# Layer 1's values by way of DRAM: tokens on partitions, and v's bias folded into the output's bias

## The chip, the cores and the metric

The kernel runs on one core of one Trainium2 chip. The metric is the device time of one execution in microseconds (us), as the median of several runs. The core's engines are TensorE (PE), VectorE (DVE), ScalarE (ACT), GpSimd (POOL) and SyncE (SP); in this kernel SP issues every DMA.

## What is computed

Thirty-two batches of 128 rows by 1024 columns pass through two layers, each an attention-like step and a low-rank expert step, each added to the running `x`:

```python
x = x + _L0_xattn_ref(_layernorm(x), ctx, ctx)       # autocorrelation along the 128 rows
x = x + _L0_ffn_ref(_layernorm(x), ...)              # dense 1024x1024 + 8 experts of rank 16, top 2
x = x + _L1_xattn_ref(_layernorm(x), ctx, ...)       # windowed attention along the 1024 columns
x = x + _L1_ffn_ref(_layernorm(x), ...)              # 4 experts of rank 16, top 2
```

The change lies in the third line. There the 128 rows are channels (8 heads of 16) and the 1024 columns are tokens. Queries come from `x`, keys and values from the context of the batch:

```python
q = Wq @ x + bq ;  k = Wk @ ctx + bk ;  v = Wv @ ctx + bv
k, v = zero padding of 8 tokens before, 7 after
for each head, token t: attn = softmax(q[t] . k[t-8 .. t+7] / 4); out[t] = sum attn * v[t-8 .. t+7]
return Wo @ out + bo
```

The padding is of zeros after the bias, so a padded token has the value 0 and not bv.

## The kernel before

**A planner sets the order.** `mk_kernel` doesn't issue instructions directly. Calls on V, A, G, PE and SP (DVE, ACT, POOL, PE, SP) are recorded as operations with a cost, the tiles they use and the earlier operations they depend on (`Planner._record`, `_touch`, `_cost`). `Planner.plan` then simulates the five engines and at each step gives a free engine its ready operation of the best priority: the batch number times a period, less the operation's remaining path, less a bias of its stage. The biases, the number of batches that may be open at a time (`win`), margins and a second set for the last part of the run stand in `CFG["plan"]`. Each engine gets its instructions in the order found; on the chip it runs them in that order, and each waits for what it needs. `emit` (line 363) issues them all, so every instruction has line 363 in the profile, and tiles tell them apart.

**Buffers.** Work tiles come from classes of fixed slots: `u` (128 x 512 f32, 43 of them), `p` (the 8 PSUM banks), `d` (128 x 1024 f32, 2), and small ones (`m`, `s`, `t`, `r`). A batch's inputs take six `u`: two halves each of `x`, of the context, and of the context split into two f16 parts. Constants and `k16`, `vpad`, `qbd` and `vbd` are there once and shared by all batches.

**A batch** passes the stages load, spec, corr, top, wt, inv (layer 0's autocorrelation, twice, for each half of the columns), ffn0 with gate and base, then kv, q, S, PV, wo (layer 1's attention) and ffn1. Several batches are open at once. The first operations of the run prepare the weights (stages setup and ws): the dense weights are loaded, their maxima found, and they are scaled and split into `wsp`.

**Products in three parts.** Most products are in f16 with each operand as a high and a low part; `three` adds high x high, high x low and low x high in one PSUM bank.

**Values before.** In `attention`, for each half of 512 tokens, `three(p, wv16, c16[g])` gives the values with channels on partitions and tokens along the row. ACT scales them and adds the bias into a `u`; ACT copies the high part into `vpad`, POOL subtracts to get the low part (`split`). `vpad` (128 x 1040 x 2 f16) holds high and low part side by side, with padding that stays zero. The product P x V needs tokens on partitions, in overlapping blocks of 32 tokens for every 16 queries. Four DVE transposes of 32 x 32 squares of 32-bit words (each word a high and a low part) per batch write them into `d` tiles. Eight DMAs copy from there into `vbd`, four for each half, one for each group of 32 channels; `vbd` is block diagonal by heads and is the stationary operand of the matmuls of stage PV. `qbd` is filled by eight DMAs for each half in the same manner from the queries, and is the stationary operand of stage S. `vbd` and `qbd` hold one half at a time.

**After PV** `eh` scales the result (each channel has its own scale for its values), `woT` multiplies it, and one DVE instruction adds `bo` and the running x (stage wo).

Of the kernel before, what the change touches and what calls it, by code (L numbers as in the profile page):

```python
# [14 lines left out]
F16 = mybir.dt.float16  # L15
# [7 lines left out]
S = 128  # L23
# [2 lines left out]
EPS = 1e-5  # L26
NEG = -3.0e38
TINY = 1e-30
CFG = {'nu': 43, 'nd': 2, 'en': 'G', 'cl': 'G', 'xl': 'G', 'sm': 'V', 'sw': 'A', 'wg': 'VG', 'q0': 'G', 'ns': 28, 'nt': 48, 'plan': {'phases': [{'at': 0.0, 'T': 19.88, 'margin': 178, 'win': 5, 'su': 60, 'sp': 3, 'ru': 1, 'rp': 0, 'bias': {'kv': -5.1, 'load': 10.0, 'S': -6.7, 'gate': 38.6, 'ffn1': 7.4, 'q': 0.4, 'top': 1.3, 'PV': -5.6, 'inv': 3.4, 'wt': 4.5, 'spec': 5.4, 'wo': 41.4, 'ws': -9.4, 'base': -1.7, 'ffn0': 90.1, 'corr': 5.4, 'setup': -12.6}}, {'at': 1459.1, 'T': 30.14, 'margin': 69, 'win': 6, 'su': 57, 'sp': 1, 'ru': 2, 'rp': 1, 'bias': {'kv': -32.9, 'load': -45.0, 'S': 18.4, 'gate': 125.0, 'ffn1': -67.8, 'q': 29.1, 'top': -23.6, 'PV': -37.2, 'inv': 57.1, 'wt': -20.7, 'spec': -56.0, 'wo': -29.3, 'ws': -71.2, 'base': -21.0, 'ffn0': 60.9, 'corr': -125.0, 'setup': 2.0}}], 'slack': [1.013, 0, 0]}}
NTOP = int(2 * math.log(S))  # L30
X_SC = 2.0 ** 10
W_SC = 2.0 ** 14
# [8 lines left out]
class _View:  # L41
# [24 lines left out]
    def broadcast_to(self, shape):  # L66
        return self._step("broadcast_to", shape)

    def windows(self, n, step, width):
        return self._step("__getitem__", (slice(None), slice(0, 1)))._wrap(n, step, width)  # L70

    def _wrap(self, n, step, width):
        f = lambda ap: bass.AP(ap.tensor, ap.offset, [list(ap.ap[0]), [step, n], [1, width]])
        return _View(self.tile, f(self.proto), self.path + ((f, None, None),))
# [7 lines left out]
    def region(self):  # L82

        ap = self.proto
        size = mybir.dt.size(ap.dtype)
        dims = [list(d) for d in ap.ap]
        row = dims[0][0]
        p0, f0 = divmod(ap.offset, row)
        last = f0 + sum(s * (n - 1) for s, n in dims[1:])
        return p0, p0 + dims[0][1], f0 * size, (last + 1) * size  # L90


class _Tile:
    def __init__(self, cls, slot=None, const=False):
        self.cls, self.slot, self.const = cls, slot, const
        self.log, self.users = [], {}


class _Op:
# [6 lines left out]
class Planner:  # L106
# [72 lines left out]
    def _cost(self, op, method, v, kw):  # L179
# [21 lines left out]
        if eng == "Activation":  # L201
            op.dur += (n + (61 if src.proto.space == PSUM else 112)) / 1.2 + 94 * (nsc + ("accum_out" in v))
            if src.region()[0] != out.region()[0]:
                op.dur += 127.0
            elif out.proto.ap[-1][0] > 1:
                op.dur += 0.2 * n
        elif eng == "DVE":
            n = max(n, size(src))
            two = method in ("tensor_copy", "tensor_scalar", "memset") and not psum and n > 64
            op.dur += 6 * n / 0.96 + 67 if method == "reciprocal" else (n * (0.5 if two else 1.0) + 64 + 59 * nsc) / 0.96  # L210
            op.dur += 70.0 * ("accum_out" in v) + {"match_replace": 67.0, "transpose": 25.0}.get(method, 0.0)
        elif eng == "Pool":
            small = mybir.dt.size(out.proto.dtype) == 2
            if method == "memset":
                op.dur += 40.0 + (0.85 if small else 0.2) * n
            else:
                rate = (2.8 if small else 1.2) if method == "tensor_scalar" else 1.88 if small else 2.1
                if any(x.proto.ap[-1][0] == 0 for x in v.values()) and n > 128:
                    rate = 1.67
                op.dur += 530.0 if kw.get("op") == ALU.pow else 150.0 + rate * n  # L220
        else:
            run = out.proto.ap[-1][1] * mybir.dt.size(out.proto.dtype)
            dram = any(x.tile is None for x in v.values())
            op.dur += (3200.0 if dram else 2900.0 if run > 128 else 3500.0) + out.shape[0] * n * mybir.dt.size(out.proto.dtype) / 360.0

            op.cold = 450.0 if dram else 720.0 if run > 128 else 840.0


    def _lat(self, a, b):
# [4 lines left out]
    def plan(self, phases, slack):  # L234
# [45 lines left out]
        while events:  # L280
            now = events[0][0]
            if phases and now >= phases[0][0]:
                period, window, margin, scarce, reserve, bias = phases.pop(0)[1]
                prio = lambda o: (period * max(o.batch, 0) - o.tail - bias.get(o.stage, 0.0), o.index)
                ready = {e: sorted((prio(o), o) for _, o in l) for e, l in ready.items()}
            while events and events[0][0] <= now:
                o = heappop(events)[2]
# [77 lines left out]

def plan_args(c):
    us = lambda v: v * 1e3
    scarce = lambda f: {"u": f["su"], "p": f["sp"], "d": 9, "m": 3, "r": 9, "s": 9, "t": 9}
# [6 lines left out]
def mk_kernel(ctx: ExitStack, tc: tile.TileContext, T: dict, out: bass.AP):  # L375
# [3 lines left out]

    cp = ctx.enter_context(tc.tile_pool(name="const", bufs=1))  # L380
    pp = ctx.enter_context(tc.tile_pool(name="psum", bufs=1, space=PSUM))

    def slot(name, shape, dt=F32):
# [98 lines left out]
    V.tensor_copy(bsum[:, 2:3], absb[:, 1:2])  # L482
    pb = B()
    PE.matmul(pb[:, 0:3], lhsT=blk1, rhs=bsum, start=True, stop=True)
    bqs, sq, bqsc, uq = (const(n, [128, 1]) for n in ("bqs", "sq", "bqsc", "uq"))
    V.tensor_scalar(bqs, pb[:, 0:1], TINY, 1.0 / W_SC, op0=ALU.add, op1=ALU.mult)
    V.reciprocal(sq, bqs)
# [4 lines left out]
    V.tensor_scalar(kvs[:, 1:2], rows[:, 2:3], C_SC / W_SC, None, op0=ALU.mult)  # L492
    V.tensor_scalar(kvb[:, 0:1], pb[:, 2:3], TINY, 1.0 / W_SC, op0=ALU.add, op1=ALU.mult)
    V.tensor_scalar(kvb[:, 1:2], absb[:, 2:3], TINY, 1.0 / W_SC, op0=ALU.add, op1=ALU.mult)
    V.tensor_scalar(rsx, rows[:, 1:3], 1.0 / W_SC, None, op0=ALU.mult)
    V.reciprocal(rsc, rsx)

    wqT = const("wqT", [128, 128])
# [321 lines left out]
    def attention(b, x, c16, m1, sums):  # L820
        P.stage = "kv"

        bd, skv, bsc, esc, usc, eh = s(2), s(2), s(2), s(2), s(1), s(2)
# [3 lines left out]
        G.tensor_tensor(bsc, bkv_raw, skv, op=ALU.mult)  # L827
# [39 lines left out]
        for g in range(2):  # L867
# [137 lines left out]
def _arrays(i):  # L1005
# [11 lines left out]
        "woT": a["L1_xattn_Wo"].T,  # L1017
# [22 lines left out]
```

## Time and profile before

| | |
|---|---|
| runs | 1600.08 us median (1599.47 to 1602.74, 3 runs) |
| the profiled execution | 1600.9 us, its span 1599.1 us |
| granted TensorE clock, mean | 0.974 |
| busy PE / DVE / ACT / POOL | 1520.9 / 1468.7 / 1417.8 / 1346.0 us |
| DMA engines, mean share | 48% (queue q1 47.8%), 142 MB in 854368 packets |
| matmuls | 19144 |

The span runs from the first to the last instruction. A busy share says how long an engine had an instruction in work, and nothing of whether another waited for it. For that there are the waits, by engine and by what ended them, and the chain of what ended last. By that chain PE holds 90% of the span, DVE 3%, ACT 2%, and the rest is in issue, DMA, POOL and SP's queue. In slices of 40 us, PE is at 9 tenths or more in all but the first two and the last two; DVE, ACT and POOL are at 8 or 9 tenths in nearly all between.

DMA pieces by size: 524288 of 32 bytes (into `qbd`), 262144 of 128 bytes (into `vbd`), 43712 of 2048 bytes (halves of 512 f32). Issuing one DMA holds SP for a median of 0.38 us (an input half) to 0.72 us (`qbd`).

### The profile page before, as it was taken

The numbers are of one execution on the slowest core, as the hardware profiler recorded it, in microseconds if no ns is written. First come the engines' busy times: TensorE is split into PE (matmuls) and PEld (weight loads), VectorE is DVE, ScalarE is ACT, GpSimd is POOL, SyncE is SP. The second block draws the span as 40 slices with busy tenths as digits, with TensorE's granted clock in tenths as the row PEclk, the third lists the DMA queues.
The fourth block names the chain that finished last, engine by engine and source line by source line (L and its number), as shares of the span: only waits on it lengthen the run. The fifth ranks groups of instructions, "written<-read, shape, count | busy, mean of one in ns | idle before, by whom it ended". The sixth has DMA issues, their size and how long they took to land.

```text
span 1599.1 us, 51794 instructions
## 1 busy us (share of the span) xinstructions
PE 1520.9 (95%) x19144; PEld 1001.9 (63%) x19144; DVE 1468.7 (92%) x5042; ACT 1417.8 (89%) x2833; POOL 1346.0 (84%) x1506
## 2 busy tenths in 40 slices
PE   2599999999999999999999999999999999999985
PEld 1256666666666666666666666666666666666654
DVE  6778999999999999999999999999999999999875
ACT  4998999999999999999999999999999999999753
POOL 5789878998888899888889988888998888899742
PEclk7789999999999999999999999999999999999996
DMA  8214544554454555445455544545455454554352
GB/s 267 81 56 57 98 63 91 102 105 91 91 91 70 94 102 106 91 91 92 69 96 101 105 91 92 93 68 96 100 105 92 90 95 68 95 100 78 41 70 58
DMA packets 854620, 145.72 MB, mean 91 GB/s; under 512 B 808224, under 2 KB 810528, under 8 KB 854368
## 3 DMA queue, kind: packets, MB, share of 16 engines
q1 hardware_dynamic: 854368, 142.41, 47.8%
q8 instruction: 152, 2.49, 0.7%
q14 instruction: 100, 0.82, 0.2%
HBM read 41.80 MB, written 16.78 MB: 37 GB/s over the span
## 4 chain that ended last, share of the span: by engine, by line
PE 90%; DVE 3%; ACT 2%; issue 1%; DMA 1%; POOL 1%; SPq 1%; POOLq 0%; DVEq 0%; ACTq 0%
PE p L363 90%; ACT u L363 2%; DVE u L363 1%; POOL u L363 1%; SPq L363 1%; DVE wsp L363 0%; DVE t L363 0%; DMA cf<-in_cf 0%; DVE s L363 0%; DMA u<-u 0%; DVE wmx L363 0%; DMA vbd<-d 0%; DVE mm L363 0%; DMA qbd<-u 0%; ACT k L363 0%
## 5 line engine op out<-in xcount | busy, mean ns | idle before, releaser
L363 POOL TENSOR_TENSOR u<-u,u 128x512 f32<-128x512 f32 (+1 forms) x640 | 774.9, 1233 | 94.4 <-ACT u L363 86.8
L363 PE MATMUL p<-wsp,u 128*128 128x512 f16 (+1 forms) x2304 | 409.9, 328 | 1.8 <-DVE r L363 0.9
L363 ACT ACTIVATE u<-p 64x512 f32<-64x512 f32 (+1 forms) x576 | 331.9, 591 | 52.0 <-PE p L363 43.7
L363 ACT ACTIVATE u<-u,t 128x512 f32<-128x512 f32 (+1 forms) x448 | 320.7, 723 | 62.3 <-DVE t L363 46.6
L363 DVE SCALAR_TENSOR_TENSOR u<-p,u 128x512 f32<-128x512 f32 (+1 forms) x448 | 289.2, 681 | 54.4 <-PE p L363 27.3
L363 PEld LDWEIGHTS <-u 128*128 128x128 f16 x3072 | 218.2, 98 | 167.0 <-issue 4.2
L363 ACT ACTIVATE u<-p,t 64x512 f32<-64x512 f32 (+3 forms) x448 | 265.7, 619 | 21.1 <-PE p L363 15.0
L363 PE MATMUL p<-u,ch 128*128 128x512 f16 x960 | 239.1, 385 | 1.9 <-DVE u L363 1.9
L363 PEld LDWEIGHTS <-qbd 128*128 128x128 f16 x6144 | 172.0, 96 | 27.1 <-issue 11.1
L363 PE MATMUL p<-k,qbd 128*128 128x32 f16 x6144 | 174.6, 176 | 1.6 <-issue 1.1
L363 PEld LDWEIGHTS <-ch 128*128 128x128 f16 x960 | 95.3, 102 | 120.7 <-issue 27.3
L363 PEld LDWEIGHTS <-vbd 128*128 128x128 f16 x6144 | 164.0, 97 | 8.5 <-issue 1.4
L363 PE MATMUL p<-u,vbd 128*128 128x32 f16 x6144 | 164.4, 176 | 0.7 <-POOL u L363 0.7
L363 ACT ACTIVATE u<-u,t,t 128x512 f32<-128x512 f32 x192 | 144.0, 820 | 5.2 <-POOL t L363 5.2
L363 POOL TENSOR_TENSOR t<-t,mhalf 128x1 f32<-128x1 f32 x128 | 71.5, 558 | 79.4 <-DVE t L363 79.0
L363 POOL TENSOR_TENSOR u<-u,s 128x512 f32<-128x512 f32 x128 | 134.2, 1050 | 0.7
L363 PE MATMUL p<-u,cf 128*128 128x512 f32 x256 | 125.2, 611 | 10.0 <-POOL u L363 10.0
L363 DVE SCALAR_TENSOR_TENSOR u<-p,t,u 128x512 f16<-128x512 f32 (+1 forms) x192 | 106.0, 567 | 16.9 <-ACT u L363 8.7
L363 ACT ACTIVATE u<-u 128x512 f16<-128x512 f32 x194 | 117.3, 623 | 3.4 <-DVE u L363 3.3
L363 PE MATMUL p<-ident,u 128*128 128x128 f32 x768 | 104.4, 279 | 10.6 <-ACT u L363 10.5
L363 PEld LDWEIGHTS p<-ident,u 128*128 128x128 f32 x768 | 90.8, 144 | 22.5 <-ACT u L363 13.4
L363 ACT ACTIVATE u<-p,t,t 128x512 f32<-128x512 f32 x128 | 94.0, 775 | 0.3 <-PE p L363 0.3
(155 smaller groups left out, 2863.8 us busy)
## 6 DMA issues: line engine op xcount, KB each, us to landing
vbd<-d SPq DMA_DIRECT2D x256, 128.0 KB
u<-u SPq DMA_DIRECT2D x192, 128.0 KB
u<-in_ctx SPq DMA_DIRECT2D x64, 256.0 KB
u<-in_x SPq DMA_DIRECT2D x64, 256.0 KB
qbd<-u SPq DMA_DIRECT2D x512, 32.0 KB
out<-u SPq DMA_DIRECT2D x64, 256.0 KB
u<-u SPq DMA_DIRECT2D x64, 126.0 KB
u<-in_wbT SPq DMA_DIRECT2D x16, 256.0 KB
```

The source lines that it names most:

```text
L363: fn(*[f(a) for a in args], **{k: f(a) for k, a in kw.items()})
```

## The change

Values are computed with tokens on partitions. The roles of the matmul's operands are exchanged: 128 tokens of the context are the stationary operand and `wv16` (128 x 128) the moving one, four blocks of tokens per half. ACT and DVE write the high and the low part, side by side, straight from PSUM into one `u`; SP stores it in a DRAM tile of 1040 rows (tokens) by 256 f16. The eight DMAs into `vbd` read their blocks from there. There are two such tiles, for even and odd batches.

Since channels now lie along the row, one scale for all channels takes the place of a scale for each: the set-up finds the largest row sum and the largest bias (`gm`). The bias bv isn't added to the values. The attention's weights add up to 1, so it is a constant, and `Wo bv + bo` is made once (`bo2`). A padded token must then hold −bv in place of 0: ACT and POOL make that row (`pads`) for each batch, and two DMAs store it ahead of the first and behind the last token.

`vpad`, the `d` tiles and the `windows` view go, and `u` has 49 slots in place of 43. The planner's cost of a DMA and its other rules are as before for all operations in this kernel; a DRAM tile counts as one region, so each store into it is planned behind the one before, and each load behind the last store. A bias may now be given for a stage on one engine too. The plan's numbers are others throughout (window 6 batches in place of 5 in the first part, the second part's set from 1484.0 us of planned time in place of 1459.1, all biases).

```diff
-CFG = {'nu': 43, 'nd': 2, ... 'plan': {'phases': [{'at': 0.0, 'T': 19.88, 'margin': 178, 'win': 5, 'su': 60, 'sp': 3, ...
+CFG = {'nu': 49, ... 'plan': {'phases': [{'at': 0.0, 'T': 20.72, 'margin': 430, 'win': 6, 'su': 101, 'sp': 99, ...
...
+    def grid(self, offset, dims):
+        f = lambda ap: bass.AP(ap.tensor, ap.offset + offset, [list(d) for d in dims])
+        return _View(self.tile, f(self.proto), self.path + ((f, None, None),))
...
-                prio = lambda o: (period * max(o.batch, 0) - o.tail - bias.get(o.stage, 0.0), o.index)
+                prio = lambda o: (period * max(o.batch, 0) - o.tail - bias.get(o.stage, 0.0) - bias.get(o.stage + "/" + o.eng, 0.0), o.index)
...
-        "d": [slot(f"d{i}", [128, D]) for i in range(CFG["nd"])],
...
+    vd = []
+    for i in range(2):
+        vd.append(P.fixed(dp.tile([D + 16, 256], F16, tag=f"vd{i}", name=f"vd{i}")))
+        vd[i].tile.whole = True
...
-    vpad = keep("vpad", [128, D + 16, 2], F16, 0.0)
...
+    bvr, nbv, bo2 = U(), const("nbv", [16, 128]), const("bo2", [128, 1])
+    SP.dma_start(out=bvr[0:16, 0:128], in_=T["bvr"].broadcast_to([16, 128]))
+    V.tensor_scalar(nbv, bvr[0:16, 0:128], -1.0, None, op0=ALU.mult)
+    PE.matmul(pb[:, 264:265], lhsT=woT, rhs=bkv_raw[:, 1:2], start=True, stop=True)
+    V.tensor_scalar(bo2, pb[:, 264:265], bo, None, op0=ALU.add)
...
-            for i, (w, hi, lo) in enumerate(((wk16, k16[:, 0, sl], k16[:, 1, sl]), (wv16, vpad[:, sl, 0], vpad[:, sl, 1]))):
-                t, p = U(), B()
-                three(p, w, c16[g])
-                A.activation(t, p, AF.Identity, bias=bsc[:, i : i + 1], scale=esc[:, i : i + 1])
-                split(hi, lo, t, G)
-
-        words = vpad.bitcast(U32).rearrange("p n i -> p (n i)")
-        v16 = []
-        for g in range(2):
-            t = P.tile("d")
-            tv = t.bitcast(U32).rearrange("p (b c) -> p b c", c=32)
-            for h in range(2):
-                V.transpose(tv[:, h * 16 : (h + 1) * 16], words[:, (2 * g + h) * 256 :].windows(16, 16, 32))
-            v16.append(h16(t).rearrange("p (b c i) -> p b c i", b=32, i=2))
+            t, p = U(), B()
+            three(p, wk16, c16[g])
+            A.activation(t, p, AF.Identity, bias=bsc, scale=esc[:, 0:1])
+            split(k16[:, 0, sl], k16[:, 1, sl], t, G)
+
+        vb = vd[b % 2]
+        t, u = M(), M()
+        pads = h16(u).rearrange("p (n r) -> p n r", r=2)
+        A.activation(t[0:16], nbv, AF.Copy, scale=skv[0:16, 1:2])
+        A.activation(pads[0:16, :, 0], nbv, AF.Copy, scale=skv[0:16, 1:2])
+        G.tensor_tensor(pads[0:16, :, 1], t[0:16], pads[0:16, :, 0], op=ALU.subtract)
+        for i in range(2):
+            SP.dma_start(out=vb[i * (D + 8) : i * (D + 8) + 8], in_=h16(u)[8 * i : 8 * i + 8])
+        for g in range(2):
+            t, p = h16(U()), B()
+            with P.group():
+                for n in range(4):
+                    for i, (m, r) in enumerate(THREE):
+                        PE.matmul(p[:, n * 128 : (n + 1) * 128], lhsT=c16[g][:, m, n * 128 : (n + 1) * 128],
+                                  rhs=wv16[:, r], start=i == 0, stop=i == 2)
+            v = t.rearrange("p (n r) -> p n r", r=2)
+            A.activation(v[:, :, 0], p, AF.Copy, scale=esc[:, 1:2])
+            V.scalar_tensor_tensor(v[:, :, 1], p, esc[:, 1:2], v[:, :, 0], op0=ALU.mult, op1=ALU.subtract)
+            SP.dma_start(out=vb[8 + g * HALF : 8 + (g + 1) * HALF].rearrange("(n p) e -> p n e", p=128),
+                         in_=t.rearrange("p (n e) -> p n e", n=4))
...
-                SP.dma_start(out=vbd[hs, :, hs], in_=v16[g][hs])
+                SP.dma_start(out=vbd[hs, :, hs].rearrange("p b n r -> p b (n r)"),
+                             in_=vb.grid(g * HALF * 256 + 64 * hp, ((256, 32), (16 * 256, 32), (1, 64))))
...
-            V.scalar_tensor_tensor(x[g], p, bo, x[g], op0=ALU.add, op1=ALU.add, accum_out=sums[:, g : g + 1])
+            V.scalar_tensor_tensor(x[g], p, bo2, x[g], op0=ALU.add, op1=ALU.add, accum_out=sums[:, g : g + 1])
```

More of the change, by code (lines that the diff above doesn't have):

```diff
@@ L28 @@
 TINY = 1e-30
-CFG = {'nu': 43, 'nd': 2, 'en': 'G', 'cl': 'G', 'xl': 'G', 'sm': 'V', 'sw': 'A', 'wg': 'VG', 'q0': 'G', 'ns': 28, 'nt': 48, 'plan': {'phases': [{'at': 0.0, 'T': 19.88, 'margin': 178, 'win': 5, 'su': 60, 'sp': 3, 'ru': 1, 'rp': 0, 'bias': {'kv': -5.1, 'load': 10.0, 'S': -6.7, 'gate': 38.6, 'ffn1': 7.4, 'q': 0.4, 'top': 1.3, 'PV': -5.6, 'inv': 3.4, 'wt': 4.5, 'spec': 5.4, 'wo': 41.4, 'ws': -9.4, 'base': -1.7, 'ffn0': 90.1, 'corr': 5.4, 'setup': -12.6}}, {'at': 1459.1, 'T': 30.14, 'margin': 69, 'win': 6, 'su': 57, 'sp': 1, 'ru': 2, 'rp': 1, 'bias': {'kv': -32.9, 'load': -45.0, 'S': 18.4, 'gate': 125.0, 'ffn1': -67.8, 'q': 29.1, 'top': -23.6, 'PV': -37.2, 'inv': 57.1, 'wt': -20.7, 'spec': -56.0, 'wo': -29.3, 'ws': -71.2, 'base': -21.0, 'ffn0': 60.9, 'corr': -125.0, 'setup': 2.0}}], 'slack': [1.013, 0, 0]}}
+CFG = {'nu': 49, 'en': 'G', 'cl': 'G', 'xl': 'G', 'sm': 'V', 'sw': 'A', 'wg': 'VG', 'q0': 'G', 'ns': 28, 'nt': 48, 'plan': {'phases': [{'at': 0.0, 'T': 20.72, 'margin': 430, 'win': 6, 'su': 101, 'sp': 99, 'ru': 1, 'rp': 0, 'bias': {'kv': -4.1, 'load': 10.2, 'S': -7.0, 'gate': 17.9, 'ffn1': 12.4, 'q': 11.5, 'top': 1.0, 'PV': -2.0, 'inv': 9.8, 'wt': 4.2, 'spec': 3.8, 'wo': 159.2, 'ws': 15.4, 'base': -0.4, 'ffn0': 56.4, 'corr': 5.2, 'setup': -7.3, 'q/SP': -14.9, 'setup/PE': 22.2, 'S/Activation': 1.9, 'load/DVE': 2.1, 'ffn1/PE': -11.8, 'corr/DVE': 13.7, 'q/Pool': 18.1, 'wt/DVE': 15.0, 'load/SP': 6.8, 'inv/Activation': 2.0, 'ffn1/DVE': 47.1, 'ffn0/Pool': -42.4, 'ffn1/Pool': 60.0, 'wo/DVE': 42.4, 'ws/SP': 21.8, 'gate/Activation': -17.3, 'load/Pool': -14.7, 'wo/PE': 3.6, 'ws/Pool': -14.6, 'wt/Activation': 6.4, 'ffn0/PE': 18.9, 'corr/PE': 3.1, 'setup/SP': 7.9, 'top/Activation': -4.1, 'PV/Activation': 2.8, 'S/PE': -0.9, 'wt/PE': 32.2, 'spec/PE': -0.2, 'setup/Activation': 3.8, 'PV/PE': 38.4, 'setup/DVE': -16.9, 'ffn0/Activation': 25.0, 'q/Activation': 0.5, 'ffn0/DVE': -32.5, 'ws/Activation': -0.2, 'gate/DVE': -8.6, 'kv/Activation': 0.9, 'top/Pool': 62.6, 'q/PE': -6.8, 'spec/SP': -42.4, 'ffn1/SP': -0.9, 'kv/DVE': 2.6, 'setup/Pool': 23.1, 'ws/DVE': 0.5, 'S/Pool': 1.2, 'gate/PE': 55.1, 'corr/Pool': 7.6, 'inv/DVE': 4.9, 'inv/Pool': 12.3, 'kv/SP': 17.4, 'S/DVE': 1.0, 'base/DVE': -33.6, 'kv/Pool': -16.4, 'PV/Pool': 7.4, 'ws/PE': 36.5, 'load/Activation': -3.5, 'ffn1/Activation': 12.6, 'PV/DVE': -6.3, 'q/DVE': -7.0, 'kv/PE': 2.2, 'spec/Activation': -0.9, 'base/PE': -1.3, 'load/PE': -0.0, 'corr/Activation': -0.0, 'inv/PE': 0.2, 'top/DVE': -0.3}}, {'at': 1484.0, 'T': 21.96, 'margin': 402, 'win': 3, 'su': 94, 'sp': 4, 'ru': 1, 'rp': 0, 'bias': {'kv': -3.6, 'load': 19.4, 'S': -7.0, 'gate': 26.8, 'ffn1': 4.1, 'q': 13.1, 'top': -4.0, 'PV': -0.3, 'inv': 9.8, 'wt': 4.5, 'spec': -6.3, 'wo': 135.3, 'ws': 17.5, 'base': -0.1, 'ffn0': 57.6, 'corr': 27.2, 'setup': -4.0, 'q/SP': -5.7, 'setup/PE': 19.1, 'S/Activation': 4.5, 'load/DVE': 2.1, 'ffn1/PE': -27.0, 'corr/DVE': 25.2, 'q/Pool': 17.4, 'wt/DVE': 12.9, 'load/SP': 6.8, 'inv/Activation': 18.3, 'ffn1/DVE': 47.2, 'ffn0/Pool': -51.2, 'ffn1/Pool': 58.8, 'wo/DVE': 34.0, 'ws/SP': 12.8, 'gate/Activation': -17.5, 'load/Pool': -4.4, 'wo/PE': 3.0, 'ws/Pool': -1.9, 'wt/Activation': 6.4, 'ffn0/PE': 30.3, 'corr/PE': 10.0, 'setup/SP': 22.3, 'top/Activation': 10.9, 'PV/Activation': 10.5, 'S/PE': -2.2, 'wt/PE': 10.2, 'spec/PE': -3.8, 'setup/Activation': 6.6, 'PV/PE': 33.3, 'setup/DVE': -3.9, 'ffn0/Activation': 42.5, 'q/Activation': -1.6, 'ffn0/DVE': -36.9, 'ws/Activation': 16.0, 'gate/DVE': -14.0, 'kv/Activation': -10.3, 'top/Pool': 62.1, 'q/PE': -7.0, 'spec/SP': -44.8, 'ffn1/SP': -0.3, 'kv/DVE': -28.5, 'setup/Pool': 23.1, 'ws/DVE': 4.1, 'S/Pool': -3.3, 'gate/PE': 57.1, 'corr/Pool': -8.3, 'inv/DVE': -1.4, 'inv/Pool': 5.1, 'kv/SP': 17.4, 'S/DVE': 5.7, 'base/DVE': -36.0, 'kv/Pool': -2.8, 'PV/Pool': -10.7, 'ws/PE': 18.8, 'load/Activation': -9.4, 'ffn1/Activation': 6.7, 'PV/DVE': -4.0, 'q/DVE': -7.0, 'kv/PE': 2.2, 'spec/Activation': 7.6, 'base/PE': -1.3, 'load/PE': -3.9, 'corr/Activation': 9.3, 'inv/PE': 22.5, 'top/DVE': -4.7}}], 'slack': [1.042, 0, 299.995]}}
@@ L67, in broadcast_to @@
         return self._step("broadcast_to", shape)
[L69 to L74, printed above, removed]
     def resolve(self):
@@ L80, in resolve @@
         return ap
+    def grid(self, offset, dims):
+        f = lambda ap: bass.AP(ap.tensor, ap.offset + offset, [list(d) for d in dims])
+        return _View(self.tile, f(self.proto), self.path + ((f, None, None),))
     def region(self):
+        if self.tile.whole:
+            return 0, 1, 0, 1
         ap = self.proto
@@ L95, in __init__ @@
         self.cls, self.slot, self.const = cls, slot, const
-        self.log, self.users = [], {}
+        self.log, self.users, self.whole = [], {}, False
 class _Op:
@@ L226, in _cost @@
             op.cold = 450.0 if dram else 720.0 if run > 128 else 840.0
+            if kw.get("transpose"):
+                op.dur, op.cold = 4400.0, 1430.0
     def _lat(self, a, b):
@@ L367, in plan_args @@
     us = lambda v: v * 1e3
-    scarce = lambda f: {"u": f["su"], "p": f["sp"], "d": 9, "m": 3, "r": 9, "s": 9, "t": 9}
+    scarce = lambda f: {"u": f["su"], "p": f["sp"], "m": 3, "r": 9, "s": 9, "t": 9}
     reserve = lambda f: {"u": f["ru"], "p": f["rp"], "m": 1, "s": 4, "t": 6}
@@ L381, in mk_kernel @@
     pp = ctx.enter_context(tc.tile_pool(name="psum", bufs=1, space=PSUM))
+    dp = ctx.enter_context(tc.tile_pool(name="dram", bufs=1, space=bass.MemoryType.DRAM))
     def slot(name, shape, dt=F32):
@@ L484, in mk_kernel @@
     PE.matmul(pb[:, 0:3], lhsT=blk1, rhs=bsum, start=True, stop=True)
+    mv, mx2, mb2, gm = const("mv", [128, 2]), s(1), M(), const("gm", [128, 2])
+    V.tensor_copy(mv[:, 0:1], rows[:, 2:3])
+    V.tensor_copy(mv[:, 1:2], absb[:, 2:3])
+    PE.transpose(pb[0:2, 128:256], mv, ident)
+    V.tensor_reduce(mx2[0:2], pb[0:2, 128:256], axis=AX.X, op=ALU.max)
+    V.tensor_copy(mb2[0:2], _bcast(mx2[0:2, 0], 128))
+    PE.matmul(pb[:, 256:258], lhsT=mb2[0:2], rhs=ident[0:2, 0:2], start=True, stop=True)
+    V.tensor_copy(gm, pb[:, 256:258])
+    bvr, nbv, bo2 = U(), const("nbv", [16, 128]), const("bo2", [128, 1])
[3 more added lines that the diff above has]
+    V.tensor_scalar(bo2, pb[:, 264:265], bo, None, op0=ALU.add)
     bqs, sq, bqsc, uq = (const(n, [128, 1]) for n in ("bqs", "sq", "bqsc", "uq"))
@@ L491, in mk_kernel @@
     V.tensor_scalar(kvs[:, 0:1], pb[:, 1:2], C_SC / W_SC, None, op0=ALU.mult)
-    V.tensor_scalar(kvs[:, 1:2], rows[:, 2:3], C_SC / W_SC, None, op0=ALU.mult)
+    V.tensor_scalar(kvs[:, 1:2], gm[:, 0:1], C_SC / W_SC, None, op0=ALU.mult)
     V.tensor_scalar(kvb[:, 0:1], pb[:, 2:3], TINY, 1.0 / W_SC, op0=ALU.add, op1=ALU.mult)
-    V.tensor_scalar(kvb[:, 1:2], absb[:, 2:3], TINY, 1.0 / W_SC, op0=ALU.add, op1=ALU.mult)
-    V.tensor_scalar(rsx, rows[:, 1:3], 1.0 / W_SC, None, op0=ALU.mult)
+    V.tensor_scalar(kvb[:, 1:2], gm[:, 1:2], TINY, 1.0 / W_SC, op0=ALU.add, op1=ALU.mult)
+    V.tensor_scalar(rsx[:, 0:1], rows[:, 1:2], 1.0 / W_SC, None, op0=ALU.mult)
+    V.tensor_scalar(rsx[:, 1:2], gm[:, 0:1], 1.0 / W_SC, None, op0=ALU.mult)
     V.reciprocal(rsc, rsx)
@@ L821, in attention @@
         P.stage = "kv"
-        bd, skv, bsc, esc, usc, eh = s(2), s(2), s(2), s(2), s(1), s(2)
+        bd, skv, bsc, esc, usc, eh = s(2), s(2), s(1), s(2), s(1), s(2)
         for i in range(2):
@@ L826, in attention @@
         V.reciprocal(skv, bd)
-        G.tensor_tensor(bsc, bkv_raw, skv, op=ALU.mult)
+        G.tensor_tensor(bsc, bkv_raw[:, 0:1], skv[:, 0:1], op=ALU.mult)
         for i in range(2):
@@ L1016, in _arrays @@
             [col(a["L1_xattn_bq"]), col(a["L1_xattn_bk"]), col(a["L1_xattn_bv"]), col(a["L1_xattn_bo"])], axis=1),
-        "woT": a["L1_xattn_Wo"].T,
+        "bvr": a["L1_xattn_bv"].reshape(1, -1), "woT": a["L1_xattn_Wo"].T,
         "ar4T": np.concatenate([a["L1_ffn_A"].reshape(64, D), a["L1_ffn_Wr"]], axis=0).T,
```

## Prediction

> **What bounds the kernel now.** I read the busy time by stage first, then the waits of each engine, the rows by shape, the timeline of one steady batch, and the chain at the end. In the table by stage each engine has its busy microseconds and instruction count, in the order PE, PEld, DVE, ACT, POOL, then granted clock, DMA share and GB/s:
>
> ```profile
> 0.00:60.00 60.00, 18.81 (x61) 10.79 (x61) 45.80 (x179) 33.90 (x64) 32.92 (x50) 0.75 0.66 208
> 60.00:215.00 155.00, 143.24 (x1398) 89.13 (x1399) 130.14 (x435) 142.06 (x278) 140.72 (x143) 0.93 0.38 71
> 215.00:1500.00 1285.00, 1284.12 (x16423) 848.55 (x16420) 1227.09 (x4259) 1190.97 (x2394) 1129.62 (x1263) 1.00 0.50 91
> 1500.00:1599.00 99.00, 74.69 (x1270) 53.45 (x1269) 65.67 (x172) 50.88 (x99) 42.70 (x53) 0.84 0.38 60
> ```
>
> From 215 to 1500 us PE is never unfed (0.9 us of 1285) and its clock is full. The waits in 300 to 1400 us say the same: PE matmuls wait for nothing, while ACT has 67 us of waits, DVE 35 and POOL 130 in those 1100. So in the middle PE sets the pace, with DVE about 1.5 us a batch behind it. A busy PE need not be PE at its peak, so I look at matmul spacing and at the period:
>
> ```profile
> 165.51 1.58 PE L363 MATMUL p<-wsp,u 128*128 128x136 f16 x24 [0.46 <-DVE u L363]
> 700.99 1.46 PE L363 MATMUL p<-wsp,u 128*128 128x512 f16 x6
> 742.95 0.92 PE L363 MATMUL p<-ar,u 128*128 128x68 f16 x24
> 708.47 0.89 SPq L363 DMA_DIRECT2D out<-u  x2
> 755.06 0.89 SPq L363 DMA_DIRECT2D out<-u  x2
> ```
>
> Six 512-wide matmuls span 1.46 us; less one latency (379 ns, row by shape) and over five steps that is 216 ns each, 2.37 columns a ns. The outputs of consecutive batches are 46.6 us apart. Thus 28 of 32 batches run at a pace that only fewer columns on PE could lower. What is left to win lies at the ends: PE is unfed for 41.2 us before 60, 11.8 before 215, 24.3 after 1500, 78 us in all, and part of what it does there runs at the lower clock.
>
> **The change, part by part.** The values' rows by shape (busy us, mean ns of one, then idle time before), and from the timeline the load of their blocks in one batch:
>
> ```profile
> L363 DVE STREAM_TRANSPOSE d<-vpad 128x512 uint32<-128x512 uint32 x128 | 88.2, 691 | 0.6 <-POOL vpad L363 0.5
> L363 POOL TENSOR_TENSOR vpad<-u,vpad 128x512 f16<-128x512 f32 x64 | 81.7, 1279 | 2.7 <-ACT vpad L363 2.7
> L363 PE MATMUL p<-u,wv 128*128 128x512 f16 x192 | 51.4, 379 | 0.0
> L363 ACT ACTIVATE vpad<-u 128x512 f16<-128x512 f32 x64 | 46.4, 811 | 0.0
> ```
>
> ```profile
> 717.98 3.87 SPq L363 DMA_DIRECT2D vbd<-d  x4
> 728.39 2.55 PE L363 MATMUL p<-u,vbd 128*128 128x32 f16 x96
> ```
>
> *PE.* Six matmuls of 512 columns a batch (wv) become 24 of 128, each with its own weight load. The same stream of load and matmul exists at 136 wide (gate, first row of the second fence: (1.58 − 0.226) / 23 = 58.9 ns) and at 68 wide ((0.92 − 0.196) / 23 = 31.5 ns); between them 128 wide gives 55.7 ns. 24 × 55.7 = 1.337 us against 6 × 216 = 1.296: +0.04 us a batch, **+1.3 us** over 32. Bounds: 0 if only columns count; 24 × 58.9 gives +3.8. This is the one term that nothing hides. The set-up's new transpose and three small matmuls (rows of 0.28 to 0.38 us) fall where PE is unfed; exposed they would be 1.5.
>
> The Trainium skill speaks against this edit: "TensorE: Matmul & The Clock Gate", Back-to-back issue gap, puts a sustained load-and-matmul stream at some 81 ns for 128 columns. By it the term would be 24 × 81 − 1296 = 0.65 us a batch, some 21 us, and the change would lose; the 58.9 ns of the gate's row, with eight columns more, disagrees, so I go by the row.
>
> *DVE.* Four transposes go (4 × 0.691 = 2.76 us a batch), two subtractions out of PSUM come (2 × 0.744, the row with a per-partition scalar): −1.27; at 1.07 (the slowest such row, into wsp) still −0.6. *ACT.* Gone are 2 × 0.775 (PSUM to u with bias) and 2 × 0.811; added 2 × 0.88 (0.686 for the f16 copy from PSUM, plus the 0.19 by which the interleaved vpad copy exceeds the plain k copy of 0.619) and two pads (0.40, the 128x128 row): −0.6. *POOL.* Gone 2 × 1.279, added one 128-wide subtraction (between 0.24 at 36 wide and 1.28): −2.1. In the middle none of the three sets the pace, so all this buys **0** there; it counts where ACT sets it, from 60 to 215 us (busy 142 of 155, PE waiting on it). There about three batches pass this stage: 3 × 0.6 = **−1.7 us** (0 to −2.9).
>
> *SP and DMA.* Four stores a batch are new: 4 × 0.55 us of issue (the u<-u row), 2.2 us. SP waits 505 of the 1100 us between 300 and 1400, 21 us a batch, so there is room. The eight vbd loads stay, 128 KB each in 128-byte pieces, but from DRAM; each now waits on SP until a store has landed, and queued behind it are the qbd loads, the spectra's copies and the outputs. In the fences: the last vbd issue ends at 721.85, PV starts at 728.39; the landing of such a load is 2.7 us on the closing chain, so some 3.8 us of slack are left. The 512-byte stores add 1024 packets × 27 ns / 16 = 1.7 us a batch per DMA engine; 128 bytes take 13 ns now and cannot exceed the 19 ns of the 272-byte DRAM loads by these rows, at most 3.1 us more. From 50% busy to 60% at most: **0**, bounds 0 to +3.3 once (a store's issue and landing, 0.6 + 2.7, at the end).
>
> A second rule against it: "DMA: Bandwidth & Descriptors", Why small descriptors are slow (HBM only), charges small pieces to HBM but not to SBUF copies. No row of this trace has 128 bytes from DRAM; by that page the load would be slower, by how much it does not say for this shape.
>
> *Buffers.* vpad and the two d tiles leave SBUF, and u goes from 43 to 49. load_batch takes exactly six u (x, c, c16, two each), and the plan's window goes from 5 to 6 batches. In the first 60 us ACT is idle for 26; 9.1 + 6.7 of these are waits for the first DMAs, which stay. Some 10 us could be filled with one more batch's work, and ACT is the engine that the next 150 us hang on. I take half, **−5** (0 to −10; −15 if the idle time after 60 closes too).
>
> *The end.* The last batch's values are made late, since there is one vpad. The timeline, and then the chain of what ended last:
>
> ```profile
> 1551.84 3.34 SPq L363 DMA_DIRECT2D vbd<-d  x4
> 1552.05 1.30 DVE L363 STREAM_TRANSPOSE d<-vpad 128x512 uint32<-128x512 uint32 x2
> ```
>
> ```profile
> 1552.48 1.25 SPq L363
> ...
> 1553.77 0.67 SPq L363
> 1554.44 0.04 issue
> 1554.48 2.71 DMA vbd<-d
> ```
>
> From 1551.84 to 1557.19 are 5.3 us in which this load decides, right behind the transposes out of vpad. With two DRAM tiles and no transposes the values can lie ready, and vbd loads as soon as PV has let it go. Then the eight qbd issues (6.2 us in the steady batch) are what is late next, so not all is won: **−3** (+3.3, as above, to −10, under half of the 24 us that PE is unfed there).
>
> *The order.* The plan's biases, margins and the start of its second phase are rewritten, so every queue's order changes. In the middle any order that keeps PE fed gives the same 46.6 us. At the ends it moves both ways and no row prices it; I take 0 and let the bounds above stand for it.
>
> *Sum*, against the profiled execution: 1600.9 (span 1599.1 and 1.8 around it) + 1.3 − 1.7 − 5 − 3 = 1592.5. The median of the runs is 0.8 below that execution: **1591.7 us**. The bias of the output (bo2 for bo) reads the same shape and costs nothing.
>
> **Rivals.** (1) *The ends do not move*: one engine's chain there is exchanged for another, extra buffers hold nothing ACT has time for. For it: ACT already has hardly a gap after 60, and the edges' chains are long sequences over all engines. Then only PE's term is left: 1600.1 + 1.3 = 1601.4, within the 0.2% (3.2 us) that a measurement of this kernel can tell from no change, or just past it.
>
> (2) *Slower: the store's landing on SP's queue reaches PE.* A vbd load may start only when PV has released vbd and the store has landed; SP is in order, so qbd waits with it. The place is the second half's PV. It decides once the load's landing is over 2.7 + 3.8 = 6.5 us after its last issue, or SP is held by that much; each further us costs 28 us in the middle. At 7 us it is 14 us more than rival 1: 1615. Against it: the 21 us of SP's waiting, the two DRAM tiles, which allow the store a batch ahead, and DMA engines half idle.
>
> (3) *128-wide matmuls cost more than the gate's row*: with every other term kept, +3.8 for +1.3 gives 1594; it ends faster still.
>
> **How the numbers follow.** Forecast with rival 3: 0.72; rival 1: 0.14; rival 2, with a worse order at the ends: 0.14. Low end: 1600.1 − 1.7 − 15 − 10 = 1573. High end: 1600.1 + 3.8 + 3.3 = 1607; beyond it lies most of rival 2. Faster by over 0.2%: 0.72; within: 0.13; slower: 0.15, which takes in a little of rival 1.
>
> **What would show it.** PE as the only engine without waits from some 220 to 1500 us and outputs still 46.6 to 46.7 us apart: the PE term. 24 wv matmuls in about 1.45 us: right; near 2 us: wrong. DVE down by about 40 us, ACT by 20, POOL by 67 in total. PE unfed for some 70 rather than 78 us at the ends, less of it before 215. Wrong if PE waits for vbd or qbd in the middle, if SP's waits name DMA stores, or if the ends lose more than they win.

## The result, and the profile after

The changed kernel takes **1607.3 us** (median of 6 runs, 1604.0 to 1608.06) against 1599.95 for the kernel before: a ratio of 1.0042, 95% interval 1.0029 to 1.0055. It is slower, by some 7 us; I had forecast 1591.7 and a range up to 1607. The profiled execution took 1607.8 us, its span 1606.0.

Busy time by stage of the changed kernel (columns as in the prediction: PE, PEld, DVE, ACT, POOL, then granted clock, DMA share, GB/s):

```profile
0.00:60.00 60.00, 16.99 (x57) 9.10 (x57) 47.66 (x152) 35.32 (x69) 31.27 (x43) 0.80 0.71 221
60.00:215.00 155.00, 142.24 (x1342) 87.78 (x1342) 128.91 (x442) 136.00 (x272) 131.38 (x144) 0.93 0.40 73
215.00:1500.00 1285.00, 1284.34 (x16965) 872.87 (x16964) 1200.67 (x4212) 1195.74 (x2393) 1074.26 (x1235) 1.00 0.60 102
1500.00:1606.00 106.00, 80.68 (x1366) 58.61 (x1364) 68.91 (x185) 52.58 (x103) 44.75 (x54) 0.85 0.43 67
```

The middle is as before: PE unfed for 0.7 us of 1285. At the ends PE is unfed for 43.0 + 12.8 + 25.3 = 81.1 us, where it was 77.3, and its busy time rose by 3.3 us (1520.9 to 1524.2). The stage m<-wqT runs once a batch; its first and last start, before and then after:

```profile
L363 ACT ACTIVATE m<-wqT,t x32: 388/402/402, 113.4 to 1536.8; 128x128 f32<-128x128 f32 x32
```

```profile
L364 ACT ACTIVATE m<-wqT,t x32: 386/402/403, 119.9 to 1543.2; 128x128 f32<-128x128 f32 x32
```

By the starts in between, the sixth batch is 3.4 us later than before (340.1, 343.5), the 28th 5.1 (1365.3, 1370.4), and the end 6.9. So in this execution the start loses 3.4 us, the 22 batches between 1.7, the end 1.8. A batch takes 46.677 us where it took 46.600.

The start in the chain of what ended last, after:

```profile
2.58 4.77 DMA u<-in_wbT
7.37 6.20 DMA u<-in_wbT
13.58 5.23 DMA u<-in_ar8T
18.84 4.54 DMA ch<-in_ch
23.42 4.80 PE p L364 x14
```

SP now issues the 16 weight loads ahead of the tables in ch, which every first matmul needs; before, ch was issued at 4.49 us and PE had 7.2 us of work done by 20. Two of the lines of PE's waits over the whole run (in total us, times, the longest us); before, none names ch:

```profile
PE p L364 <- DVE t L364: 21.7, 5, 13.2
PE p L364 <- DMA ch<-in_ch: 17.5, 1, 17.5
```

The rows of the values after (busy us, mean ns):

```profile
L364 ACT ACTIVATE u<-p,t 128x512 f16<-128x512 f32 x128 | 97.0, 761 | 5.4 <-DVE t L364 1.7 <-PE p L364 0.7
L364 DVE SCALAR_TENSOR_TENSOR u<-p,t,u 128x512 f16<-128x512 f32 x128 | 95.5, 767 | 3.1 <-ACT u L364 1.8 <-POOL m L364 1.1
L364 PE MATMUL p<-wv,u 128*128 128x128 f16 x768 | 53.2, 219 | 0.0
L364 POOL TENSOR_TENSOR m<-m,m 16x128 f16<-16x128 f32 x32 | 14.6, 455 | 14.4 <-ACT m L364 11.7 <-DMA vbd<-vd 2.7
L364 ACT ACTIVATE m<-nbv,t 16x128 f16<-16x128 f32 x32 | 13.4, 418 | 0.2 <-DVE t L364 0.2
```

Half of the first two rows' 128 were there before (43.8 and 47.4 us), so the values cost ACT 53 us and the pads 26, DVE 48, POOL 15, and the transposes' 88 us, the vpad copies' 46, the vpad subtractions' 82 and half of ACT's 94 for scaling with a bias are gone. The code does what it says. The time went elsewhere.

### The profile page after: what moved, and what is told of

The parts are those of the page before. It is cut to its first block, busy times and chain, and to the rows that moved or that the text cites. A ratio compares the mean times of both kernels' runs of the same rounds, so it can differ in the third digit from the quotient of the medians.

```text
span 1606.0 us, 52930 instructions
## 1 busy us (share of the span) xinstructions
PE 1524.2 (95%) x19725; PEld 1028.4 (64%) x19725; DVE 1446.1 (90%) x4986; ACT 1419.7 (88%) x2833; POOL 1281.7 (80%) x1473
## 4 chain that ended last, share of the span: by engine, by line
PE 91%; DVE 3%; ACT 3%; DMA 1%; issue 1%; POOL 1%; SPq 0%; POOLq 0%; ACTq 0%; DVEq 0%
PE p L364 91%; ACT u L364 2%; DVE u L364 1%; DVE wsp L364 1%; DMA u<-in_wbT 1%; POOL u L364 0%; DMA u<-in_ar8T 0%; DVE t L364 0%; DMA ch<-in_ch 0%; DVE s L364 0%; DVE mm L364 0%; DMA u<-u 0%; POOL bl L364 0%; DVE ar L364 0%; SPq L364 0%
## 5 line engine op out<-in xcount | busy, mean ns | idle before, releaser
L364 PEld LDWEIGHTS <-u 128*128 128x128 f16 x3840 | 271.1, 98 | 180.8 <-issue 4.4
L364 ACT ACTIVATE u<-p,t 64x512 f32<-64x512 f32 (+3 forms) x512 | 317.7, 646 | 42.2 <-PE p L364 32.8
L364 ACT ACTIVATE u<-u,t 128x512 f32<-128x512 f32 (+1 forms) x448 | 308.0, 713 | 42.7 <-DVE t L364 20.7
L364 PE MATMUL p<-u,ch 128*128 128x512 f16 x960 | 236.9, 389 | 22.8 <-DMA ch<-in_ch 17.5
L364 PE MATMUL p<-u,vbd 128*128 128x32 f16 x6144 | 169.3, 177 | 3.3 <-ACT u L364 2.2
L364 PEld LDWEIGHTS <-ch 128*128 128x128 f16 x960 | 91.8, 102 | 122.0 <-issue 24.3
L364 DVE SCALAR_TENSOR_TENSOR u<-p,t,u 128x512 f16<-128x512 f32 (+1 forms) x256 | 152.1, 622 | 16.3 <-ACT u L364 14.6
L364 DVE TENSOR_REDUCE s<-p 128x16 f32<-128x512 f32 x128 | 88.3, 690 | 38.5 <-PE p L364 38.5
```

The costliest lines, as they stand in the source:

```text
L364: fn(*[f(a) for a in args], **{k: f(a) for k, a in kw.items()})
```

## The experiments

Theory A: the time is lost in the order at the two ends that the new plan numbers make, and narrow matmuls cost what their spacing says. The rivals: B, the narrow matmuls; C, the wait for the store's landing; D, a start that hangs on the weights, wherever the tables stand; E, the new code costs time at the ends in any order. All ratios are to the kernel before on the same chip, with 95% intervals; its median there was 1601.0 for the first four, 1600.2 for the next four, 1601.7 for the last two.

**Wide matmuls in the changed kernel.** The order of all engines is kept (the recorded operation only issues other calls).

```diff
+            P.ops[-1].calls = [
+                (nc.tensor.matmul, (p,), dict(lhsT=wv16[:, m], rhs=c16[g][:, r], start=i == 0, stop=i == 2))
+                for i, (m, r) in enumerate(THREE)]
```

> The changed kernel with every engine's order kept, but each half's values made by 3 matmuls of 512 columns in place of 12 of 128 (the values are then laid out wrongly; nothing else is left out). Theory A (the loss lies in the order at the ends, the narrow matmuls cost what their spacing says): 24 x 55.8 ns against 6 x 215.8 is 0.044 us a batch, so 1.4 us less than the changed kernel, 1606. Theory B (the narrow matmuls are the loss, with stalls that their spacing hides): the whole distance of 7 us back, 1600. Theory C (the DRAM round trip is the loss): as A.

1604.7 us, ratio 1.0025 (1.0014 to 1.0035): some 2.7 us less than the changed kernel, between A and B and nearer A; most of the loss stays. A batch takes 46.591 us here. PE's time a batch, from start to start by what is multiplied (mean of 22 batches, ns):

| | before | wide in the changed kernel | changed |
|---|---|---|---|
| values (wv) | 1295 | 1295 | 1340 |
| S (k, qbd) | 4850 | 4856 | 4898 |
| inverse transforms (cf as right side) | 3517 | 3034 | 3034 |
| ffn1's last product (b4) | 1014 | 1327 | 1326 |
| q (wqs) | 1800 | 1883 | 1883 |
| all | 46600 | 46591 | 46677 |

The narrow matmuls cost 45 ns a batch, 1.4 us in all. The rest of the difference is three single stalls inside stage S (0.09, 0.74 and 0.28 us from one matmul to the next, at 369, 696 and 743 us) that the profile puts to no other engine. The shipped order, that of the changed kernel, is also that of this run and the next and, but for two loads, of the one after. These four have 13 such stalls of over 0.08 us between 215 and 1500 us, up to 1.05 us long: one in this run, three in the changed kernel, five and four in the other two. The kernel before has none. All 13 lie at the same place of PE's own program: within two instructions of number 192 of each 256, all of PE's instructions counted from the start. That program comes on a DMA queue of its own, in 156 pieces of 16 KB for 39952 instructions (152 for 38980 in the kernel before), which is one piece for 256; the changed kernel's page has (pieces, MB, share):

```profile
q8 instruction: 156, 2.56, 0.7%
```

Each time PE went on 2.4 to 2.8 us after such a piece had begun. So at these places PE waited for its own instructions, for 1 us in all in the changed kernel. The other rows show that the new order moves waits between products and gains nothing by it.

**No wait for the store.**

```diff
+                fn, args, kw = P.ops[-1].calls[0]
+                vz = T["vz"]
+                kw = dict(kw, in_=bass.AP(vz.tensor, g * HALF * 256 + 64 * hp, [[256, 32], [16 * 256, 32], [1, 64]]))
+                P.ops[-1].calls = [(fn, args, kw)]
```

> The changed kernel with every engine's order kept; the loads into vbd read a constant DRAM array of the same size instead of the tile that was just stored, so that no load waits for a store (the stores are still made, and the attention's values are then constants). Theory A (order at the ends): nothing, 1607 within 1 us, and PE still without waits in the middle. Theory C (the wait for the store's landing holds SP's queue): several of the 7 us come back, 1600 to 1604.

1606.4 us, ratio 1.0036 (1.0023 to 1.0050), a batch 46.70 us: within its interval the changed kernel. In the changed kernel itself the waits of SP from 300 to 1400 us name no store either. Theory C, which was my rival for slower, falls.

**The tables early.**

```diff
+    early = [o for o in P.order if o.batch < 0 and o.what == "dma_start" and o.calls[0][2]["in_"] in (T["ch"], T["cf"])]
+    rest = [o for o in P.order if o not in early]
+    at = 1 + max(i for i, o in enumerate(rest) if o.eng == "SP" and o.start < 2500.0)
+    P.order = rest[:at] + early + rest[at:]
```

> The changed kernel with one edit of SP's order: the loads of ch and cf, which stand behind the 16 loads of in_wbT and issue at 18.8 us, go ahead of all but two of these (some 4 us). Theory A (SP's order in the first 25 us is what the start loses): PE's first matmuls start some 10 us earlier, and 2 to 4 us of the 7 come back, 1603 to 1605. Theory D (the start hangs on the weights' preparation on DVE and ACT, wherever the tables stand): 0 within 1 us, or a little slower, since the weights come 0.9 us later.

1607.1 us, ratio 1.0040 (1.0027 to 1.0052): nothing. The load of ch is issued at 3.53 us in place of 18.84. The first two stages of 20 us, in the changed kernel and then here:

```profile
0.00:20.00 20.00, 0.56 (x2) 0.50 (x2) 12.60 (x25) 6.60 (x10) 14.33 (x26) 1.00 0.95 304
20.00:40.00 20.00, 6.98 (x25) 3.08 (x25) 15.06 (x51) 13.51 (x26) 4.16 (x4) 0.85 0.96 296
```

```profile
0.00:20.00 20.00, 5.31 (x14) 2.04 (x14) 12.53 (x25) 9.19 (x15) 14.32 (x26) 1.00 0.94 320
20.00:40.00 20.00, 4.72 (x13) 2.24 (x13) 15.71 (x55) 11.75 (x23) 5.41 (x5) 0.54 0.95 300
```

PE starts early, and then waits for DVE and ACT: it had 17.5 us of waiting for ch to lose, and lost none of the run's time by it. So the most striking wait of the new profile was not the cause; what theory A expected of this run falls, and theory D holds for this edit. A wait that ends before the stage's true limit costs nothing, also when it is the longest single one in the table.

**Relief without a new order, in the kernel before.**

```diff
                 split(hi, lo, t, G)
+                if i and b >= 4:
+                    P.ops[-1].calls = P.ops[-2].calls = []
...
                 V.transpose(tv[:, h * 16 : (h + 1) * 16], words[:, (2 * g + h) * 256 :].windows(16, 16, 32))
+                if b >= 4:
+                    P.ops[-1].calls = []
```

> The kernel before with every engine's order kept, but from the fifth batch on without the ACT copy into vpad, the POOL subtraction and the four DVE transposes (the attention then uses the old contents of d for its values): relief of 1.6, 2.6 and 2.8 us a batch, more than the change brings, at no cost. If the middle hangs on PE alone: 0 there, and at the end up to 3 us less, since the last loads into vbd wait for no transposes: 1597 to 1600. If DVE, ACT or POOL share the pace of the middle: over 5 us less, below 1595.

1599.3 us, ratio 0.9989 (0.9980 to 0.9998): 1.7 us less. A batch takes 46.62 us, so 7 us of relief a batch buy nothing in the middle, as priced. From the 28th batch's m<-wqT to the end it takes 230.9 us where it took 233.9: the end is shorter by 3 us, which is the size that I had put down for it. It does not come by way of the load into vbd, as I had priced it. These are PE's lines around the first PV that uses the load of 1551.84, in the kernel before and then here:

```profile
1560.08 1.97 PE L363 MATMUL p<-ident,u 128*128 128x128 f32 x8 [1.62 <-ACT u L363]
1561.84 0.23 PE L363 MATMUL p<-u,vbd 128*128 128x32 f16 x1
1562.54 2.70 PE L363 MATMUL p<-u,vbd 128*128 128x32 f16 x95 [0.46 <-POOL u L363]
```

```profile
1559.16 1.97 PE L363 MATMUL p<-ident,u 128*128 128x128 f32 x8 [2.31 <-ACT u L363]
1560.92 0.23 PE L363 MATMUL p<-u,vbd 128*128 128x32 f16 x1
1561.62 2.68 PE L363 MATMUL p<-u,vbd 128*128 128x32 f16 x95 [0.47 <-POOL u L363]
```

By the prediction's chain the load had landed at 1557.19, and PE came to it 4.7 us later, after waits for ACT and with one for POOL to come. Here the load's issue starts at 1548.39, 3.4 us earlier, and PV only 0.9 us earlier. So the gain at the end was real, but by the relief of the engines and not by this load; which of the three gave it wasn't tried. And an order has to collect it.

**The changed code with the old plan numbers**, with 49 and with 43 u slots:

```diff
-CFG = {'nu': 49, ... 'plan': {'phases': [{'at': 0.0, 'T': 20.72, 'margin': 430, 'win': 6, ...
+CFG = {'nu': 49, ... 'plan': {'phases': [{'at': 0.0, 'T': 19.88, 'margin': 178, 'win': 5, ...
```

> The changed kernel's code and its 49 u slots, with the plan's numbers of the kernel before (window, margins, biases, both parts). The order that the planner makes of it is a new one. Theory A (the numbers of the new plan lose the time at the ends, the code does not): clearly below the changed kernel, 1600 or less. Theory E (any order pays, because the new code is harder to fit in, or the plan's numbers suit only the code they were set for): above 1607; the planner's own simulation ends 12 us later than for the kernel before, which would give 1612.

> As the run with 49 u slots, with 43: code and old plan alone, without the freed buffers. My prediction priced the six slots at 5 us (0 to 15): then this is 5 us slower than the run with 49. If slots hold nothing ACT has time for (rival 1): the same within 2 us. The planner's own simulation puts 13 us between them.

1612.2 us, ratio 1.0077 (1.0065 to 1.0090), with 49 slots, and 1628.0, ratio 1.0174 (1.0160 to 1.0188), with 43. The numbers belong to the code they were set for: theory A's first prediction here is wrong. With 49 slots the loss is not at the start: by m<-wqT the sixth batch is 2.2 us ahead of the kernel before (337.9 and 340.1), the 27th 1.5 behind, and the end 10.9 behind. And six slots are worth 16 us with these numbers, though each count of slots gets an order of its own. Where, shows in the second and the last stage (49 slots, then 43):

```profile
60.00:215.00 155.00, 141.72 (x1407) 89.22 (x1408) 129.55 (x431) 143.94 (x285) 135.44 (x142) 0.93 0.40 72
1500.00:1610.00 110.00, 79.57 (x1269) 55.39 (x1268) 66.39 (x175) 50.47 (x99) 40.68 (x51) 0.80 0.44 64
```

```profile
60.00:215.00 155.00, 132.87 (x1288) 82.63 (x1289) 122.09 (x394) 134.53 (x270) 128.38 (x138) 0.91 0.37 74
1500.00:1626.10 126.10, 95.89 (x1504) 67.54 (x1502) 81.44 (x219) 63.41 (x123) 52.75 (x64) 0.85 0.42 63
```

With 43 all four engines do 7 to 9 us less between 60 and 215 us, and PE has 16 us more left after 1500.

**Narrow matmuls in the kernel before**, its order kept:

```diff
+                if i:
+                    P.ops[-1].calls = [
+                        (nc.tensor.matmul, (p[:, n * 128 : (n + 1) * 128],),
+                         dict(lhsT=w[:, m], rhs=c16[g][:, r, n * 128 : (n + 1) * 128], start=j == 0, stop=j == 2))
+                        for n in range(4) for j, (m, r) in enumerate(THREE)]
```

> The kernel before with every engine's order kept; each half's values are made by 12 matmuls of 128 columns in place of 3 of 512, with the same result. Theory A (narrow matmuls cost their spacing): 32 x 0.045 = 1.4 us more than the kernel before. Theory B (they cost twice that, by stalls behind them as the first run with wide matmuls hinted, 2.6 us): 2.5 us or more. By the 81 ns for a load and matmul of 128 columns that the Trainium skill states (TensorE: Matmul & The Clock Gate, Back-to-back issue gap) it would be 21 us more.

1600.7 us, ratio 1.0004 (0.9995 to 1.0013): between −0.8 and +2.1 us. The profile has 1340 ns a batch for the values, as in the changed kernel. Theory B's 2.5 us lies outside. The estimate of 21 us from the 81 ns of the Trainium skill ("TensorE: Matmul & The Clock Gate", Back-to-back issue gap) lies far outside.

**The changed code in another order.** The plan's numbers were searched by random steps, from the old ones, for an early end in the planner's own simulation.

```diff
-CFG = {'nu': 49, ... 'phases': [{'at': 0.0, 'T': 20.72, 'margin': 430, 'win': 6, 'su': 101, 'sp': 99, ...
+CFG = {'nu': 49, ... 'phases': [{'at': 0.0, 'T': 19.56, 'margin': 88, 'win': 6, 'su': 13, 'sp': 6, ...
```

> The changed kernel's code with 49 u slots and plan numbers searched anew from those of the kernel before, to end early in the planner's own simulation, 14.8 us before that of the changed kernel and 6.3 before that of the kernel before. Theory A (order at the ends): the start and the end shrink, the middle keeps its 46.6 to 46.7 us a batch: 1590 to 1598. Theory E (the code itself costs time at the ends): 1603 or more.

**1595.1 us**, ratio 0.9971 (0.9960 to 0.9981): 11 to 12 us under the changed kernel with the same instructions and slots, and 5 under the kernel before. Its first two stages, and its m<-wqT:

```profile
0.00:60.00 60.00, 24.58 (x82) 13.16 (x83) 46.48 (x170) 38.62 (x73) 38.72 (x52) 0.78 0.65 204
60.00:215.00 155.00, 144.39 (x1497) 92.34 (x1496) 138.19 (x486) 145.85 (x297) 135.08 (x146) 0.95 0.49 95
```

```profile
L364 ACT ACTIVATE m<-wqT,t x32: 373/401/403, 107.0 to 1529.0; 128x128 f32<-128x128 f32 x32
```

PE is unfed for 35.4 us in the first 60 (43.0 in the changed kernel), with ACT and POOL busier by 3 and 7 us, and the whole run is some 13 us ahead from the first batch on. That start is the whole gain: the end (from the 29th batch, 188.7 us against 189.1) and the middle (46.71 us a batch) are not better. Theory E falls.

**Is it the search or the code?** The kernel before and the changed code with 43 slots, each with plan numbers searched in the same way; the bias for a stage on one engine is allowed in both:

```diff
-CFG = {'nu': 43, 'nd': 2, ... 'phases': [{'at': 0.0, 'T': 19.88, 'margin': 178, 'win': 5, ...
+CFG = {'nu': 43, 'nd': 2, ... 'phases': [{'at': 0.0, 'T': 19.88, 'margin': 259, 'win': 5, ...
...
-CFG = {'nu': 49, ... 'phases': [{'at': 0.0, 'T': 20.72, 'margin': 430, 'win': 6, ...
+CFG = {'nu': 43, ... 'phases': [{'at': 0.0, 'T': 19.88, 'margin': 46, 'win': 5, ...
```

> The kernel before with its 43 u slots and plan numbers searched anew in the same way and at about twice the length (a bias for a stage on one engine allowed here too); the planner's own simulation ends 2.6 us earlier than for the kernel before. If the search alone made the 5 us of the changed code with its new order: 1595 or less here too. If the changed code and its slots made them: 1596.5 to 1600.

> The changed code with 43 u slots and plan numbers searched anew for it; the planner's own simulation ends 8.8 us later than with 49. If the slots carry the gain (the term I priced at 5 us): 1601 to 1606, the kernel before or slower. If relief of DVE, ACT and POOL carries it: as with 49, 1595 to 1598.

1599.7 us, ratio 0.9985 (0.9976 to 0.9993), for the old code, and 1607.0, ratio 1.0037 (1.0023 to 1.0051), for the changed code with 43. The search alone gives the old code 2.4 us (1.1 to 3.8), and the changed code with all its slots comes out 2 us lower still; the two intervals overlap a little, so that difference is likely but not certain. Without the slots the changed code loses some 11 us. So with these orders what the change has to give sits in the freed SBUF. Each of the three stands for one search, and a search of another length could find orders that shift these numbers.

The planner's own simulated end puts these kernels in their measured order, but for two that the measurement can't tell apart (the changed kernel, and the changed code with 43 slots in its new order). Simulated and measured us: kernel before 1563.0 and 1600.0, its new order 1560.4 and 1599.7, changed code 1571.5 and 1607.3, old numbers with 49 slots 1574.8 and 1612.2, with 43 1588.0 and 1628.0, new order 1556.7 and 1595.1, with 43 1565.5 and 1607.0. The distance is 36 to 42 us in all. For the change itself the model says 8.5 us slower, and 7.3 were measured. The changed kernel's number is not quite on the scale of the others: its plan counts DVE, ACT and POOL at 1.042 of the model's cost and a DMA of a batch 0.3 us longer, the other plans count 1.013 and nothing (`slack` in `CFG`). Its order taken as it is, with the others' figures, ends at 1569.5, which is still in its place.

## Why the prediction was wrong

- **PE.** Right: +1.3 us forecast at 55.7 ns, 1340 − 1295 = 45 ns a batch measured, 1.4 us, at 55.8 ns from start to start. The rule of 81 ns ("TensorE: Matmul & The Clock Gate", Back-to-back issue gap) doesn't hold for this stream. PE's waits for its own instructions, 1 us in all, came on top. The 1.5 us of the set-up that this paragraph of the prediction names entered neither the sum nor the high end of the range.
- **DVE, ACT, POOL.** In the rows of the values right: by mean times counts DVE −38, ACT −22 and POOL −67 us (forecast −40, −20, −67); the pads cost ACT 0.80 us a batch and the interleaved copy 0.84. The totals of the page changed by −23 on DVE, −64 on POOL and +2 on ACT. They count time once in which two instructions of an engine overlap. The durations themselves add up to 25 us less on DVE, 68 less on POOL and 46 less on ACT (1636.4 and 1590.7 us), so ACT's instructions are shorter in all and overlap less in the new order. That the relief buys nothing in the middle is shown by the run with relief alone. The −1.7 us at the start was not found in the shipped order.
- **SP and DMA.** Right that it costs nothing: without the wait for the store the time is the same, and the DMA share from 215 to 1500 us went from 50% to 60%, as bounded. The 128-byte pieces do take longer from DRAM: 90% of them ended within 13 ns before and within 26 ns now, and their sum per DMA engine rose from 201 to 268 us. This agrees in direction with the Trainium skill's "DMA: Bandwidth & Descriptors", Why small descriptors are slow (HBM only); PE doesn't see it.
- **Buffers, −5.** The term exists and is larger than I put it (16 and 11 us between 43 and 49 slots in two pairs of orders; in the searched order the sixth batch is 10.8 us ahead of the kernel before), but I took it as given with the slots. In the shipped order PE is unfed for 43.0 us of the first 60, more than before.
- **The end, −3.** The 3 us are there in the old order, but by luck of size. The reading "5.3 us in which this load decides" was wrong: PE came to the loaded values 4.7 us after they had landed. In the chain the landing is followed by a POOL instruction (t<-t,mhalf, of a layer norm) that doesn't read vbd, and I took the step for a cause. The shipped order loses 1.8 at the end instead.
- **The order, 0.** This is the step that failed: "At the ends it moves both ways and no row prices it; I take 0 and let the bounds above stand for it." Same instructions, same buffers, another order: 1595.1 in place of 1607.3. An order is worth at least 11 us here, more than the 8.4 of all my other terms together; with 0 and no bound of its own, both the forecast and the high end of the range came out too low. My terms for buffers and end were worked out from the old order's gaps, as if the new one would fill them.
- **The rivals.** Rival 1, ends that do not move, was nearest, at 1601.4. Rival 2 had the sign and the wrong cause; its chance of 0.14 took in "a worse order at the ends", the only place where the order's loss appears, without a price.

What stays open: which part of the shipped order loses the start and the end. In the changed kernel's profile the sixth batch is 3.4 us late, in the three runs that keep its order, one of them but for the tables, 1.2 to 1.8, so the split between start, middle and end varies between executions. Moving the tables alone doesn't mend it; no smaller edit of the order was tried, nor the plan's larger slack by itself.

## What to carry to other kernels

When one engine is fed without a gap for 80% of the run, relief of the others can pay only at the start and the end, and there an instruction saved is worth what the order makes of it. A change that comes with a new order is two changes: price the order by itself, with both signs, or compare codes only when each has an order made for it. If the kernel carries a model that made its order, ask it for the new program's end: here it said 8.5 us slower where the gaps of the old order said 8.4 faster. And a step in the chain of what ended last is an inference: before a wait is priced, look whether the instruction behind it reads what was waited for.

## What the runs showed of the hardware

- 128-column f16 matmuls with a weight load each start 55.8 ns apart at full clock, with the context or with the weights as stationary operand, against 215.8 ns for 512 columns.
- 128-byte pieces from DRAM: median 13 ns as from SBUF, but 26 ns at 90% and 53 at 99%, where copies within SBUF had 13.
- PE's program arrives in pieces of 16 KB, one for 256 instructions. In stage S, where a load and matmul start every 25 ns, PE stood for up to 1.05 us at the edge of a piece: 13 times in four runs of one order, never in the kernel before.
- The longest single wait in PE's table, 17.5 us for one load, could be taken away with no effect on the run's time.
